# A weight load moved one step earlier in the DMA queue, and three idle products moved behind a kernel's first transposes

## The chip, the cores and the metric

The kernel runs on one core of a Trainium2 chip. A core has five engines that run their own instruction streams: TensorE (matrix products; PE, with its weight loads listed as PEld), VectorE (DVE), ScalarE (ACT), GpSimd (POOL) and SyncE (SP), which in this kernel issues all DMA transfers of the main part. The metric is the device time of one execution in microseconds (us); less is better. Times inside the program are counted from the start of the profiled span.

## The reference

The reference is a stack of two transformer layers on `x` of shape (16, 256, 256), with a condition vector per sample (16, 256) and a context (16, 256, 192). Everything is float32.

```python
# layer 0: 16 heads of width 64, rotary positions on q and k
attn_in = adaln(x, cond, ...)              # layernorm * (1 + cond@gw) + cond@bw
x = attn(attn_in, attn_in, ...) + x        # self attention
cross_in = adaln(x, cond, ...)             # the same modulation again
x = attn(cross_in, ln(context), ...) + x   # cross attention
x = gelu(adaln2(x) @ w1) @ w2 + x          # feed-forward
# layer 1: 16 heads of width 16, scale and shift from silu(cond) @ Wmod
x = x + attn(h1 @ Wqkv) @ Wos
x = x + attn(h2 @ Wq, context @ Wk, context @ Wv) @ Woc
x = x + gelu(h3 @ W1) @ W2
```

So there are six phases (layer 0: self attention, cross attention, feed-forward; layer 1: the same), each for 16 samples. A phase has its own weights.

## The kernel before, in words

**Order of work.** The 16 samples of `x` stay in SBUF for the whole run. A job is one phase of one sample: 6 x 16 = 96 jobs, phase by phase. An attention job has two steps (`s` = 0 and 1), each for half of the heads; a feed-forward job has four. One Python loop over all steps writes the instructions of every engine in the order in which they run (a manual schedule: nothing reorders them). A step holds work of several jobs at once: softmax sums and weighted sums of the current job, rotary projections of the next step, the output product of the job before, and the preparation of jobs one to three places ahead.

**One layer-0 attention step on TensorE** is, in this order: projections of keys and queries for the next step (`stage_rotary`, products recorded at L82), weighted sums of values (`layer0_sums`, L611), in step 0 the values of the next job (`layer0_values`, L82 and, for cross attention, L445 too; in step 1 the output product of the job before), and the scores of the next step (`stage_s`, L542). Behind the scores, a coming step of cross attention starts its keys (L478). DVE multiplies projections by the rotary tables (L499), POOL combines the two halves to `qk` (L507), ACT takes the exponential (L554) and copies out of PSUM (L618, L451). The helper `product` (L82) issues each product as four of 32 output rows.

**The sums of the softmax.** `sum_up` turns the row sums into reciprocals `inv` (L585), SP writes them to DRAM (`sums_seen`, L588) and reads them back spread over the partitions (`spread`, L591); POOL multiplies the raw outputs by them (L600) and forms folded sums (L709) for an output product in the manner of Strassen, whose results DVE adds to `x` (L723 to L730).

**Transfers.** All of them go through SP's one queue, strictly in program order; an instruction of SP that waits holds all behind it. A job's normalized input is transposed by DVE and turned through DRAM: `turned` (L326) out, `fetched` (L336) back; the context of cross attention goes the same way (`turned_c` L349, `fetched_c` L360), and its tile becomes `cT`.

**Weights of the next phase** come by `load_phase(p, part)`. For layer-0 attention the parts are "early" (output weights and bias), "first" and "last" (one half each of key and query weights, L228 and L229) and "values" (the value weights, two transfers of 512 KB, L236). The value weights have a single buffer (`wv`): cross attention's `wv_ca` can be written only when TensorE has read self attention's `wv_sa` for the last time. That is in `layer0_values` of the last self-attention job (b = 15), which stands in step 0 of the job before it (b = 14). The condition `leaving` holds in the two steps of the last sample of a layer-0 attention phase.

**The beginning.** `condition()` transposes the condition vectors and the table of bias rows (L154) on TensorE. Between them stand `idle_products`: products of the identity matrix (128 x 128 by 128 x 256, L136) into PSUM bank 0, whose results nobody reads. Then the first modulation (`modulation`, eight products at L175, five DVE instructions L182 to L186), four transposes of the first normalized sample (L859), and `prepare_input`, where ACT (L369) and DVE (L370) write one half each of `hT`, the input of the first projections.

Of the kernel before, what the change touches and what calls it, by code (L numbers as in the profile page):

```python
# [43 lines left out]
def fast(ctx: ExitStack, tc: tile.TileContext, a: dict, out: bass.AP, flag):  # L44
# [5 lines left out]
    NB = a["x"].shape[0]  # L50
# [13 lines left out]
    def bank(i, *inner):  # L64

        flat = banks[:, i, :]
        if len(inner) == 1:
            return flat[:, 0 : inner[0]]
        return flat[:, 0 : inner[0] * inner[1]].rearrange("p (a n) -> p a n", n=inner[1])
# [41 lines left out]
    def column(name, c):  # L111
        r, _, w = row_of[name]
        return cols[0:w, r + c : r + c + 1]
# [13 lines left out]
    def transpose_condition(s, src):  # L127
        pc = bank(5 + s, KC, NB)
        for c in range(KC):
            nc.tensor.transpose(pc[:, c, :], src[:, c * P : (c + 1) * P], ident[:NB, :NB])  # L130
        nc.vector.tensor_copy(condT[:, s], pc)

    def idle_products(n):

        for _ in range(n):
            nc.tensor.matmul(  # L136
                bank(0, 2, P), ident, ident.unsqueeze(1).to_broadcast([P, 2, P]), start=True, stop=True
            )

    def condition():  # L140

        sig = work.tile([NB, D], F32, tag="inv", name="sig")
        nc.scalar.activation(sig, cond, AF.Sigmoid)
        soon = stat.tile([NB, 1], F32, tag="ve", name="soon")
        nc.scalar.activation(soon, cond[:, 0:1], AF.Exp)
        silu = work.tile([NB, D], F32, tag="inv", name="silu")
        idle_products(1)
        transpose_condition(0, cond)
        nc.vector.tensor_mul(silu, sig, cond)
        idle_products(1)  # L150
        transpose_condition(1, silu)
        idle_products(2)
        pr = bank(4, n_rows)
        nc.tensor.transpose(pr, rows, ident[:n_rows, :n_rows])  # L154
        idle_products(1)
        return pr

    def load_modulation(shift_w, scale_w, name, between=None):
# [207 lines left out]
    def affine(pt, cw, scale, bias, tag, name, eng=nc.gpsimd):  # L366

        dst = work.tile([cw, 2, N], F32, tag=tag, name=name)
        nc.scalar.activation(dst[:, 0, :], pt[:, 0, :], AF.Identity, bias=bias(0), scale=scale(0))  # L369
        eng.tensor_scalar(dst[:, 1, :], pt[:, 1, :], scale(1), bias(1), ALU.mult, ALU.add)  # L370
        return dst
# [41 lines left out]
    def prepare_input(job):  # L413

        b, key = job["b"], job["key"]
        factor, addend = job["phase"]["mod"]
        job["hT"] = hT = affine(
            job.pop("hraw"), P,
            lambda c: factor[:, c, b : b + 1], lambda c: addend[:, c, b : b + 1], "hT", f"hT_{key}",
            nc.vector if b == 0 and job["p"] == 0 else nc.gpsimd,  # L420
        )
        if not job["cross"]:
            job["kT"] = hT
        elif job["layer"] == 0:
            job["kT"] = affine(
                job.pop("craw"), P,
                lambda c: column("L0_xcond_ca_lnc_w", c), lambda c: column("L0_xcond_ca_lnc_b", c),
                "cT", f"cT_{key}",
            )
# [368 lines left out]
    def load_phase(p, part):  # L798
        ph = phases[p]
        if part == "early" and ph["layer"] == 0 and p > 0:  # L800
            ph["make_mod"] = ph["mod_load"]() if ph["mod_load"] else lambda at: phases[p - 1]["mod"]
        ph.setdefault("w", {}).update(ph["load"](part))
# [3 lines left out]
    for p, ph in enumerate(phases):  # L806
        for b in range(NB):
            job = {"phase": ph, "p": p, "layer": ph["layer"], "kind": ph["kind"], "cross": ph["cross"], "b": b,
                   "key": f"{p}_{b}", "index": len(jobs), "qk": {}, "pr": {}, "turns": [], "raw": [], "parts": [], "halves": [],
                   "last": p == len(phases) - 1}  # L810
# [38 lines left out]


    pr = condition()
    jobs[0]["hraw"] = bank(7, KC, N)
    found = moments(xs[0], "first")
# [3 lines left out]
    for c in range(KC):  # L857
        for t in range(NT):
            nc.tensor.transpose(  # L859
                jobs[0]["hraw"][:, c, t * P : (t + 1) * P], xh[:, t, c * P : (c + 1) * P], ident  # L860
            )
    prepare_input(jobs[0])
    for e in range(2):
        for half in range(2):
# [11 lines left out]
    for i, (j, s) in enumerate(steps):  # L876
        job = jobs[j]
        ffn, layer0 = job["kind"] == "ffn", job["layer"] == 0
# [8 lines left out]
        if s == 1 and job["b"] == (3 if ffn else 1) and more:  # L887
            load_phase(job["p"] + 1, "early")
            if job["layer"] == 1:
                for part in ("first", "last"):  # L890
                    load_phase(job["p"] + 1, part)
        leaving = layer0 and not ffn and job["b"] == NB - 1
        if leaving and s == 0:
            for part in ("first", "values"):
                load_phase(job["p"] + 1, part)
        if layer0 and not ffn and s == 1 and job["b"] == 2:
            make_mod = phases[job["p"] + 1]

# [731 lines left out]
```

## Time and profile before

| what | before |
|---|---|
| device time, three runs | 2203.62, 2204.10, 2205.29 us; median 2204.1 |
| the profiled execution | 2205.85 us as timed, span 2204.0 us |
| mean granted TensorE clock in it | 0.999 of full |
| PE busy | 2186.9 us (99%) |
| DVE / POOL / ACT busy | 1663.7 (75%) / 1071.4 (49%) / 837.7 us (38%) |
| DMA | 117.69 MB, mean 53 GB/s |
| self attention of layer 0 ends, cross attention begins | near 670 to 690 us |

The profile is one execution on the chip. A row of its timeline has the start, the length, the engine, the line of the kernel, the operation with what it writes and reads (`out<-in`), shapes, and how many instructions are merged; square brackets give the engine's idle time in front and what ended it. A float32 product shows as two records, so a product by `product` (four parts) shows as eight. Rows overlap a little, since products are pipelined; the distance between starts is the safer measure. A row of a list of windows gives the length of the window, the busy time of PE, PEld, DVE, ACT and POOL in it with counts, then the granted TensorE clock, the busy share of the DMA engines and GB/s.

### The profile page before, as it was taken

What the parts mean: (1) busy time and instruction counts of PE and PEld (TensorE: products, weight loads), DVE (VectorE), ACT (ScalarE), POOL (GpSimd) and SP (SyncE); (2) the same over time, 40 slices, a digit from 0 to 9 for tenths busy, and PEclk for the clock granted to TensorE, in tenths of its full rate; (3) what the DMA queues carried; (4) which work ended last, traced back from release to release, by engine and by line L of the source; (5) the groups of instructions that cost most, each with busy time, mean ns of one, the idle gap of its engine ahead of it and who ended that gap; (6) DMA issues with size and microseconds to landing.
All of it is one profiled execution on the core that took longest, in us unless ns stands there. A gap on an engine that the chain in (4) does not pass through costs nothing.

```text
span 2204.0 us, 110738 instructions
## 1 busy us (share of the span) xinstructions
PE 2186.9 (99%) x50501; PEld 1460.3 (66%) x50501; DVE 1663.7 (75%) x3116; ACT 837.7 (38%) x1303; POOL 1071.4 (49%) x1033
## 2 busy tenths in 40 slices
PE   9999999999999999999999999999999999999998
PEld 5666666666655666666665667776656566558998
DVE  5886776776787898889899875554777777777654
ACT  3323323323323323333333332224666666663322
POOL 3766656666656867676776751221232332322220
PEclk9999999999999999999999999999999999999999
DMA  6110110111132221222212123221222232223221
GB/s 191 46 40 22 25 40 22 24 40 22 28 82 72 66 61 39 50 50 42 58 34 60 25 72 87 49 45 28 65 42 42 50 96 60 61 51 86 61 63 36
DMA packets 306248, 117.69 MB, mean 53 GB/s; under 512 B 242580, under 2 KB 289001, under 8 KB 305641
## 3 DMA queue, kind: packets, MB, share of 16 engines
q1 hardware_dynamic: 305768, 110.51, 21.0%
q8 instruction: 397, 6.50, 1.3%
q14 instruction: 83, 0.67, 0.1%
HBM read 77.14 MB, written 33.29 MB: 50 GB/s over the span
## 4 chain that ended last, share of the span: by engine, by line
PE 95%; POOL 1%; DVE 1%; DMA 1%; issue 1%; ACT 0%; SPq 0%; DVEq 0%; POOLq 0%; ACTq 0%
PE banks L82 62%; PE banks L542 16%; PE banks L611 9%; PE banks L627 5%; PE banks L478 1%; PE banks L445 1%; POOL raw L600 1%; PE banks L175 0%; DVE m L499 0%; POOL qk L507 0%; DMA sums_seen<-inv 0%; POOL folded L709 0%; ACT pr L554 0%; DMA rows<-in_rows 0%; DMA spread<-sums_seen 0%
## 5 line engine op out<-in xcount | busy, mean ns | idle before, releaser
L554 ACT ACTIVATE pr<-banks 128x1024 f32<-128x1024 f32 x576 | 487.8, 937 | 411.3 <-PE banks L542 207.9
L507 POOL TENSOR_TENSOR qk<-m,m 128x512 f32<-128x512 f32 x256 | 347.6, 1378 | 305.3 <-DVE m L499 208.1
L499 DVE TENSOR_TENSOR m<-banks,rope 128x512 f32<-128x512 f32 x512 | 324.0, 678 | 81.1 <-POOL qk L507 75.4
L563 DVE TENSOR_TENSOR both<-pr 128x512 f32<-128x512 f32 x256 | 224.6, 890 | 109.9 <-ACT pr L554 109.4
L618 ACT COPY raw<-banks 128x512 f32<-128x512 f32 x128 | 75.2, 587 | 473.4 <-PE banks L611 467.3
L542 PE MATMUL banks<-qk 32*64 32x256 f32 x8192 | 241.5, 378 | 2.3 <-DVE x L726 1.4
L611 PE MATMUL banks<-pr,v 128*32 128x256 f32 x4096 | 233.2, 379 | 0.0
L542 PEld LDWEIGHTS banks<-qk 32*64 32x64 f32 x8192 | 184.9, 131 | 63.0 <-issue 23.2
L677 ACT ACTIVATE g<-banks,cols 128x256 f32<-128x256 f32 x256 | 107.2, 471 | 294.4 <-PE banks L82 275.7
L611 PEld LDWEIGHTS banks<-pr,v 128*32 128x32 f32 x4096 | 133.1, 110 | 88.4 <-ACT pr L554 0.7
L600 POOL TENSOR_TENSOR raw<-raw,spread 128x512 f32<-128x512 f32 x128 | 164.2, 1317 | 21.1 <-DMA spread<-sums_seen 15.0
L82 PE MATMUL banks<-folded_w,folded 128*32 128x128 f32 x5856 | 173.1, 273 | 0.0
L569 DVE STREAM_TRANSPOSE squares<-both 128x1024 f32<-128x1024 f32 x128 | 159.4, 1246 | 4.4
L82 PEld LDWEIGHTS banks<-folded_w,folded 128*32 128x32 f32 x5856 | 162.5, 110 | 0.1
L576 DVE TENSOR_REDUCE rows<-squares 128x32 f32<-128x1024 f32 x128 | 155.4, 1214 | 2.2
L662 POOL TENSOR_TENSOR oT<-oT,spread 128x256 f32<-128x256 f32 x64 | 45.8, 738 | 210.7 <-DVE spread L661 210.7
L303 POOL TENSOR_TENSOR rstd<-ve,neg_half 128x2 f32<-128x2 f32 x95 | 75.3, 792 | 144.3 <-DVE ve L301 141.0
L82 PE MATMUL banks<-hT,wk_sa 128*32 128x256 f32 x2048 | 136.1, 384 | 0.9 <-ACT hT L369 0.9
L627 PE MATMUL banks<-pr,wide_v 128*32 128x256 f32 x2048 | 134.4, 379 | 1.1 <-ACT pr L554 1.1
L82 PE MATMUL banks<-hT,wq_sa 128*32 128x256 f32 x2048 | 134.8, 381 | 0.0
L82 PE MATMUL banks<-hT,wq_ca 128*32 128x256 f32 x2048 | 134.0, 379 | 0.0
L396 POOL TENSOR_TENSOR x<-x,bo_b 128x256 f32<-128x256 f32 x96 | 73.2, 782 | 124.5 <-DVE xh L311 124.5
(154 smaller groups left out, 3680.7 us busy)
## 6 DMA issues: line engine op xcount, KB each, us to landing
turned<-blocks SPq DMA_DIRECT2D x380, 64.0 KB
fetched<-turned SPq DMA_DIRECT2D x380, 64.0 KB
spread<-sums_seen SPq DMA_DIRECT2D x128, 128.0 KB
x<-in_x SPq DMA_DIRECT2D x16, 256.0 KB
fetched_c<-turned_c SPq DMA_DIRECT2D x64, 64.0 KB
cT<-in_ctx_turned SPq DMA_DIRECT2D x16, 256.0 KB
out<-x SPq DMA_DIRECT2D x16, 256.0 KB
ctx<-in_ctx SPq DMA_DIRECT2D x16, 192.0 KB
```

The lines of the kernel that those rows point to most:

```text
L82: nc.tensor.matmul(out[cut], lhsT[:, cut], rhs, start=start, stop=stop)
L499: nc.vector.tensor_tensor(m, pq, rope[:, s : s + 1, :].to_broadcast([P, 2, N]), ALU.mult)
L507: nc.gpsimd.tensor_tensor(r, x, y, (ALU.subtract, ALU.add)[out])
L542: nc.tensor.matmul(banks[64 * g : 64 * g + 64, at + h, t * N : (t + 1) * N], lhs, rhs, start=(half == 0), stop=(half == 1 or job["layer"] ...
L554: nc.scalar.activation(pr[:, one], sc[:, one], AF.Exp, scale=0.125 if job["layer"] == 0 else 0.25)
L563: nc.vector.tensor_tensor(job["both"][:, 2 * p : 2 * p + 2, :], pr[:, :, 0, :], pr[:, :, 1, :], ALU.add)
L569: nc.vector.transpose(job["squares"].rearrange("p b k -> p (b k)"), job.pop("both").rearrange("p h n -> p (h n)"))
L576: nc.vector.tensor_reduce(job["rows"][:, u, :], job.pop("squares"), AX.X, ALU.add)
L600: nc.gpsimd.tensor_tensor(part, part, spread[:, u : u + 1, :].to_broadcast([P, 2, N]), ALU.mult)
L611: nc.tensor.matmul(o[32 * h : 32 * h + 32, half, :], v[:, t, col : col + 32], prs[h // 2][:, h % 2, t, :], start=(t == 0), stop=(t == NT - 1),
L627: nc.tensor.matmul(o[32 * h : 32 * h + 32], v[:, t, 4 * c + h, 32 * e : 32 * e + 32], prs[h // 2][:, h % 2, t, :], start=(t == 0), stop=(t ...
L677: nc.scalar.activation(g[:, c, :], ph[:, c, :], AF.Gelu, bias=column(w["b1"], 2 * u + c))
```

## The change

Two things move; nothing is computed differently.

1. `load_phase(..., "values")` of the next layer-0 phase is now called in step 1 of the job b = 14. Before, it was called one step later, in step 0 of b = 15, together with "first". In SP's queue the two `wv_ca` transfers so stand directly behind `fetched_c` of cross attention's first job, and ahead of `turned` and `turned_c` of its second job (four transfers each) and of the first halves of the key and query weights (`wk_ca`, `wq_ca`), which they followed before. The same condition holds at the end of cross attention, where the next phase is the feed-forward, which has no "values" part, so nothing is issued.
2. The idle product that stood between the transpose of the bias rows and the first modulation is gone, and three stand between the four transposes of the first sample and the first projections.

The other engines' instructions and their order are the same.

```diff
@@ condition()
         idle_products(2)
         pr = bank(4, n_rows)
         nc.tensor.transpose(pr, rows, ident[:n_rows, :n_rows])
-        idle_products(1)
         return pr
@@ the beginning, behind the modulation
             nc.tensor.transpose(
                 jobs[0]["hraw"][:, c, t * P : (t + 1) * P], xh[:, t, c * P : (c + 1) * P], ident
             )
+    idle_products(3)
     prepare_input(jobs[0])
@@ the loop over steps
         leaving = layer0 and not ffn and job["b"] == NB - 1
+        if layer0 and not ffn and job["b"] == NB - 2 and s == 1:
+            load_phase(job["p"] + 1, "values")
         if leaving and s == 0:
-            for part in ("first", "values"):
-                load_phase(job["p"] + 1, part)
+            load_phase(job["p"] + 1, "first")
```

## The prediction

> **What bounds the kernel now.** I read the page's busy shares first, then who TensorE waits for, then the two stretches in which it stands.
>
> ```profile
> PE 2186.9 (99%) x50501; PEld 1460.3 (66%) x50501; DVE 1663.7 (75%) x3116; ACT 837.7 (38%) x1303; POOL 1071.4 (49%) x1033
> PE banks L82 <- DMA wv_ca<-in_ca_wkv: 2.9, 1, 2.9
> PE banks L542 <- DVE x L726: 1.4, 2, 0.8
> ```
>
> TensorE is busy 2186.9 of 2204.0 us, so only its 17 us of idle time and products that run slowly can be won. Its longest wait in the whole run (second line: who waited, for what, us, times, longest) is for `wv_ca`, cross attention's value weights. The timeline shows the place, and one stage later the same work without the wait:
>
> ```profile
> 653.48 0.98 SPq L236 DMA_DIRECT2D wv_ca<-in_ca_wkv x2
> 653.37 3.64 PE L611 MATMUL banks<-pr,v 128*32 128x256 f32 x64
> 659.92 4.97 PE L82 MATMUL banks<-wv_ca,cT 128*32 128x512 f32 x32 [2.92 <-DMA wv_ca<-in_ca_wkv]
> 666.70 3.71 PE L542 MATMUL banks<-qk 32*64 32x256 f32 x128
> 698.00 3.64 PE L611 MATMUL banks<-pr,v 128*32 128x256 f32 x64
> 706.87 3.71 PE L542 MATMUL banks<-qk 32*64 32x256 f32 x128
> ```
>
> From the weighted sums (L611) to the next scores (L542) the disturbed passage takes 666.70 - 653.37 = 13.33 us, the clean one 706.87 - 698.00 = 8.87. **4.46 us** are lost: 2.92 idle and about 1.5 because the products then ran slowly. Fine windows (last three columns: granted clock, DMA share, GB/s) show the clock:
>
> ```profile
> 659.00:659.50 0.50, 0.00 (x0) 0.00 (x0) 0.47 (x2) 0.00 (x0) 0.50 (x1) 0.74 1.05 406
> 660.00:660.50 0.50, 0.50 (x4) 0.13 (x8) 0.50 (x2) 0.00 (x0) 0.00 (x0) 0.50 1.06 370
> 662.50:663.00 0.50, 0.50 (x9) 0.19 (x5) 0.47 (x4) 0.00 (x0) 0.00 (x0) 0.85 0.00 0
> ```
>
> Means of 0.74 and 0.85 put the drop to one half at 659.24 and the return at 662.65.
>
> The start is slow too, though the clock column says 1.00 there:
>
> ```profile
> 6.85 1.16 PE L136 MATMUL banks<-ident 128*128 128x256 f32 x2
> 7.80 3.43 PE L175 MATMUL banks<-condT,mod_a 128*128 128x16 f32 x16
> 11.08 1.09 PE L859 MATMUL banks<-ident,xh_first 128*128 128x128 f32 x4
> 13.08 1.94 PE L82 MATMUL banks<-hT,wk_sa 128*32 128x256 f32 x16 [0.91 <-ACT hT L369]
> 17.88 1.04 PE L82 MATMUL banks<-hT,wq_sa 128*32 128x256 f32 x16
> 793.26 1.82 PE L175 MATMUL banks<-condT,mod_a 128*128 128x16 f32 x15
> ```
>
> A modulation takes 3.43 us here and 1.82 at 793 us; two projections take 1.71 (13.08 to 14.79, where the query group begins) and 0.86 after 17.88 (next group at 18.74). The projection begun at 17.35 takes 0.53, between the two, so full speed begins at about 17.56.
>
> [...] 659.24 to 662.65 is 3.41, and 659.24 - 17.56 = 641.68 is 188 times 3.413. [...] Here 16 KB of `sums_seen` issued at 655.67 let its reader go only at 662.16 (6.50 us in the chain), against 1.72 from issue to issue at 611.09.
>
> **Part 1, the value weights.** Two DMAs of 512 KB move ahead of ten others in SP's queue: four `turned_1`, four `turned_c_1`, `wk_ca` and `wq_ca`. Their new place is behind `fetched_c`, whose issue ends at 618.30. The load waits there for TensorE's last read of `wv_sa` in the same buffer; those products run from 615.51 until the scores at 622.49. SP's next work is `turned_1` at 645.16, so a blocked SP for 4 us holds nobody. One MB at the 300 to 400 GB/s of 657 to 661 us takes about 3 us; nothing else moves from 622.5 to 645. The data are there near 626 to 628 for a use at 656.8: 29 us to spare. The context (`cT`) is there too, its second half made at 646.39 in 0.56. The banks are free: the last evacuation of the sums ends at 657.66 (bank 5), and values take banks 6 and 7 first. Gain: **4.46**.
>
> What is late next? The stage's other long chain is also on DMA: reciprocal `inv` ready at 652.60, `sums_seen` issued at 655.67, spread from 662.22, POOL's multiply (L600) at 667.91, three foldings, `rstd`, rotary subtraction, DVE's update of x, and TensorE standing for a bank (0.60 + 0.31 us at 688.87 and 689.79, "PE banks L542 <- DVE x L726" and L730). TensorE arrives there 4.46 earlier, so the chain must move too: it costs nothing more if POOL's multiply starts by 667.91 - 4.46 - 0.91 = 662.5. It does move: the two weight issues (0.98) leave the queue, so `sums_seen` goes at about 654.6, with 1.2 MB ahead of it instead of 2.3. At the 230 to 300 GB/s seen in that stretch, from 653.5, that is 657.7 to 658.8, plus 1.0 for the small write and its signal: spread from 658.7 to 659.8. It lands 3.5 later, an estimate from 512 KB at the 225 GB/s of 614 us plus its issue. So POOL starts at 662.2 to 663.3 and the present 0.91 becomes 0 to 0.8: **gain 0.1 to 0.9; I take 0.3**. In a quiet stage POOL has 3.77 us of idle time before its next rotary work (632.34), which covers the rest of the lateness.
>
> **Part 2, the idle products.** One is taken from in front of the modulation, three are added behind the transposes. Price of one at half speed: 7.80 - 6.85 = 0.95. The modulation starts at 6.87 and not 7.80 (its weights were issued before `rows`, which is in by 6.68; that they are in too is an inference). Everything up to the transposes moves by 0.93: they end at 11.04 (11.97 before), and ACT's half of hT at 12.10 instead of 13.03. Three products last until 11.04 + 2.85 = 13.89, so the first projection comes **0.81 later** than now. Behind it stand all projections, DVE's rotary, the values; none else has a deadline there: scores at 29.16 wait for POOL's qk, done at 26.96.
>
> In return TensorE stands nowhere behind 11.04. [...] With the profiled phase [...] full speed comes at 14.15. Before: 4.48 us of half speed are 2.24 of work. After: 13.89 to 14.15 does 0.13, the other 2.11 end at 16.26. Gain 17.56 - 16.26 = 1.30. [...] mean **+0.6**. Bounds: -0.5 [...] to +1.6.
>
> **Sum.** 4.46 + 0.3 + 0.6 = 5.4 us off the profiled execution's 2204.0 span (2205.85 as timed, 1.85 around the span). The three plain runs have a median of 2204.1; I take the same amount off it: **2198.7**. Nothing else changes on DVE, ACT or POOL; with TensorE 99% busy, what it gains early stays to the end as long as its later waits hang on its own progress, as the one at 767 (0.8 + 0.3) does.
>
> **Rivals.**
> (a) The stall moves to the update of x. For it: the chain's two DMA steps are what TensorE meets next, and the present trace already shows 0.91 there. Against: two of the four 512 KB loads ahead of them leave. If POOL's multiply still started at 667.91, the stand would be 0.91 + 4.46 and only part 2 would be left: 2204.1 - 0.6 = 2203.5; at half the move, about 2201.3.
> (b) The change doesn't do what it says: the load is still issued late, or something else of that step is late (context, banks). Against: the tiles' times above. Then 2203.5.
> (c) Slower: SP, in order, blocks on the buffer's release, and `turned_1` and `sums_seen` stand behind it. From a release after about 656 (652.60 plus the 3.8 of slack) each us costs one; it must eat the 5.4 and 4.4 more, so it decides from about 666, and would give 2208.5 or more. For it: a DMA is moved in front of ten others of a strict queue. Against: the last reader in the trace ends at 622.5.
> (d) The start as in the bad phase in most runs: -0.4, so 4.46 + 0.3 - 0.4 = 4.4 and 2199.7.
>
> **Chances.** A difference of 0.2% (4.4 us) is about what a measurement can tell from none. Forecast with the good start 0.53 (2197.4 to 2199.2); (d) 0.30 (2199.0 to 2200.4); (a) 0.09; (b) 0.03; (c) 0.03; more gain than 7 us, from a chain that moves further, 0.02. Faster by over 0.2%: 0.53 + 0.02 + half of (d) and 0.03 of (a), 0.73; within: 0.24; slower: 0.03. The range that leaves out no more than 2 in 10, with the ends of the unknown costs: 2196.8 to 2201.2.
>
> **What would show it.** `wv_ca` issued near 622.5 and no wait of TensorE for it; no half clock near 659; L611 to L542 in 8.9 us. POOL's L600 of that stage some 5 us earlier, and the wait on L726 there below 0.6. First modulation product near 6.9, first projection near 13.9, full speed near 14 (or, in the bad phase, later than 16). Wrong if TensorE stands for L726 or L730 by several us, if SP holds `turned_1`, or if three idle products don't bring full speed earlier.

## The result, and the profile after

| | before | changed |
|---|---|---|
| median of 22 runs each | 2204.73 us (2201.58 to 2206.99) | 2200.59 us (2198.65 to 2203.05) |
| ratio | | 0.9981, 95% interval 0.9975 to 0.9988 |
| profiled execution, as timed / span | 2205.85 / 2204.0 us | 2200.25 / 2198.4 us |
| PE busy | 2186.9 us | 2184.9 us |

The change gains 4.1 us (2.6 to 5.5), 0.19%. The two profiled executions differ by 5.6 in their spans; how much more this is than the medians' difference, and where it lies, is told below. Between the first and the second hunk the lines of the changed kernel are lower by one (L542 became L541).

Two rows of what TensorE waits for, from the changed kernel (who, for what, us in total, times, longest):

```profile
PE banks L541 <- DVE x L725: 1.6, 2, 1.0
PE banks L541 <- DVE x L729: 0.6, 2, 0.3
```

The wait for `wv_ca` (2.9) is gone from the list. The one on DVE's update of x, 1.4 before, has become 1.6. The timeline of the changed kernel shows the load, the passage that was disturbed, and the chain behind it:

```profile
622.26 0.91 SPq L235 DMA_DIRECT2D wv_ca<-in_ca_wkv  x2
651.89 0.34 DVE L584 RECIPROCAL inv<-banks 128x32 f32<-128x32 f32 x1
653.01 3.64 PE L610 MATMUL banks<-pr,v 128*32 128x256 f32 x64
653.41 0.41 SPq L587 DMA_DIRECT2D sums_seen<-inv  x1
656.46 3.62 PE L82 MATMUL banks<-wv_ca,cT 128*32 128x512 f32 x32
658.52 2.02 SPq L590 DMA_DIRECT2D spread<-sums_seen  x4
661.89 3.71 PE L541 MATMUL banks<-qk 32*64 32x256 f32 x128
663.55 5.90 POOL L599 TENSOR_TENSOR raw<-raw,spread 128x512 f32<-128x512 f32 x4 [4.37 <-DMA spread<-sums_seen]
671.79 3.64 PE L610 MATMUL banks<-pr,v 128*32 128x256 f32 x64
681.67 1.98 PE L541 MATMUL banks<-qk 32*64 32x256 f32 x64
684.64 0.61 PE L541 MATMUL banks<-qk 32*64 32x256 f32 x2 [0.99 <-DVE x L725]
685.57 1.98 PE L541 MATMUL banks<-qk 32*64 32x256 f32 x62 [0.31 <-DVE x L729]
687.48 1.09 PE L477 MATMUL banks<-cT,wk_ca 64*64 64x256 f32 x16
```

The load is issued at 622.26, right after the last read of `wv_sa`. From the weighted sums to the next scores it is 661.89 - 653.01 = 8.88 us; it was 13.33. Two wide windows of the changed kernel (granted clock third from the end) show no slow clock any more:

```profile
655.00:660.00 5.00, 5.00 (x64) 1.77 (x56) 4.93 (x6) 1.17 (x2) 2.69 (x3) 1.00 0.52 176
660.00:665.00 5.00, 5.00 (x138) 3.25 (x142) 2.10 (x11) 3.05 (x6) 1.45 (x2) 1.00 0.81 238
```

So 4.45 us are won in this passage. Behind it more is lost than before: at the update of x TensorE stands (is held up; such a wait is called a stand below) for 0.99 + 0.31 us, where it stood for 0.60 + 0.31. The same place in the kernel before:

```profile
676.60 3.64 PE L611 MATMUL banks<-pr,v 128*32 128x256 f32 x64
686.28 1.98 PE L542 MATMUL banks<-qk 32*64 32x256 f32 x64
688.87 0.61 PE L542 MATMUL banks<-qk 32*64 32x256 f32 x2 [0.60 <-DVE x L726]
689.79 1.98 PE L542 MATMUL banks<-qk 32*64 32x256 f32 x62 [0.31 <-DVE x L730]
691.70 1.09 PE L478 MATMUL banks<-cT,wk_ca 64*64 64x256 f32 x16
```

The start, from the timeline of the changed kernel:

```profile
6.86 0.38 PE L154 MATMUL banks<-ident,rows 68*128 68x68 f32 x1 [0.50 <-DMA rows<-in_rows]
7.03 3.53 PE L174 MATMUL banks<-condT,mod_a 128*128 128x16 f32 x16
10.40 1.09 PE L858 MATMUL banks<-ident,xh_first 128*128 128x128 f32 x4
11.29 2.77 PE L136 MATMUL banks<-ident 128*128 128x256 f32 x6
13.98 1.91 PE L82 MATMUL banks<-hT,wk_sa 128*32 128x256 f32 x16
15.69 1.07 PE L82 MATMUL banks<-hT,wq_sa 128*32 128x256 f32 x16
16.59 1.04 PE L82 MATMUL banks<-hT,wk_sa 128*32 128x256 f32 x16
28.73 1.55 PE L541 MATMUL banks<-qk 32*64 32x256 f32 x48
```

The modulation follows the bias rows after 0.17 us (1.12 before). The first projection comes at 13.98, 0.90 later than before, but only the first group (15.69 - 13.98 = 1.71) is at half speed; the next takes 0.90. The first scores come at 28.73, against 29.16.

### The profile page after: what moved, and what is told of

It reads as the page before. It is cut to its first block, busy times and chain, and to the rows that moved or that the text cites. A ratio compares the mean times of both kernels' runs of the same rounds, so it can differ in the third digit from the quotient of the medians.

```text
span 2198.4 us, 110747 instructions
## 1 busy us (share of the span) xinstructions
PE 2184.9 (99%) x50505; PEld 1435.8 (65%) x50505; DVE 1662.3 (76%) x3116; ACT 836.9 (38%) x1303; POOL 1070.4 (49%) x1033
## 4 chain that ended last, share of the span: by engine, by line
PE 93%; POOL 2%; DVE 2%; DMA 1%; issue 1%; SPq 0%; ACT 0%; DVEq 0%; POOLq 0%; ACTq 0%
PE banks L82 61%; PE banks L541 15%; PE banks L610 9%; PE banks L626 5%; PE banks L477 1%; PE banks L444 1%; POOL raw L599 1%; DVE m L498 1%; POOL folded L708 1%; PE banks L174 0%; POOL qk L506 0%; DMA sums_seen<-inv 0%; DMA spread<-sums_seen 0%; ACT pr L553 0%; DMA rows<-in_rows 0%
## 5 line engine op out<-in xcount | busy, mean ns | idle before, releaser
L541 PE MATMUL banks<-qk 32*64 32x256 f32 x8192 | 240.6, 378 | 2.5 <-DVE x L725 1.6
L541 PEld LDWEIGHTS banks<-qk 32*64 32x64 f32 x8192 | 185.0, 131 | 62.2 <-issue 24.8
```

Source lines behind the costliest of these rows:

```text
L541: nc.tensor.matmul(banks[64 * g : 64 * g + 64, at + h, t * N : (t + 1) * N], lhs, rhs, start=(half == 0), stop=(half == 1 or job["layer"] ...
```

## The experiments

Two theories of the sum stood against each other at first: A, that the fetch is worth about 4 us and the idle products some tenths with a clear sign; B, that the idle products are worth nothing. Then Q, that the remaining stand at the update of x comes from the DMA queue, against P, that POOL and DVE slow each other down. All runs in one table; each ratio is to the kernel before on the same chip.

| kernel | median us (runs) | ratio | 95% interval |
|---|---|---|---|
| value weights alone | 2200.10 (14) | 0.9982 | 0.9974 to 0.9990 |
| idle products alone | 2203.16 (13) | 0.9995 | 0.9986 to 1.0003 |
| no idle products | 2199.35 (15) | 0.9978 | 0.9970 to 0.9986 |
| one idle product | 2198.65 (9) | 0.9975 | 0.9965 to 0.9985 |
| six idle products | 2200.34 (16) | 0.9981 | 0.9974 to 0.9988 |
| first halves early | 2196.79 (6) | 0.9968 | 0.9956 to 0.9980 |
| first halves early, one idle product | 2196.92 (5) | 0.9965 | 0.9951 to 0.9978 |
| first halves early, values not | 2200.18 (8) | 0.9979 | 0.9969 to 0.9990 |

### The two parts, each alone

Value weights alone: the kernel before with the last hunk of the change. Idle products alone: the changed kernel with that hunk taken back:

```diff
-        if layer0 and not ffn and job["b"] == NB - 2 and s == 1:
-            load_phase(job["p"] + 1, "values")
         if leaving and s == 0:
-            load_phase(job["p"] + 1, "first")
+            for part in ("first", "values"):
+                load_phase(job["p"] + 1, part)
```

> The kernel before with part 1 alone (the value weights' load one step earlier), the idle products as they were. Theory A (the fetch gives 4.4 us by itself and hands 0.4 back at the update of x; the idle products give about +0.6 in the mean): ratio 0.9982, 4.0 us less than before, TensorE never waits for wv_ca, clock 1.00 through 655 to 665 us, the waits on L726 and L730 at the update near 685 together 1.2 to 1.4 us. Theory B (the idle products are worth nothing or cost a little, and the fetch is the whole of the 4.1): the same or up to 0.4 us more than that. If the two parts were of one size, 2 us each, ratio 0.9991.

> The kernel before with part 2 alone (the idle products behind the modulation and transposes). Theory A: mean gain 0.6 us, ratio 0.9997 (0.9994 to 1.0000); in its trace the first projection at 13.9 to 14.0[...]; the wait of 2.9 us for wv_ca stays as it was. Theory B: ratio 1.0000 to 1.0002, since a later start takes back what earlier full speed gives.

The value weights alone gain 4.0 us (2204.56 x 0.0018; 2.2 to 5.7; the medians differ by 4.5), practically the whole change, and as theory A had it (theory B's time is so near that this run alone doesn't part the two). In that kernel's trace the passage from sums to scores takes 661.32 - 652.45 = 8.87 us, and at the update of x TensorE stands for 0.99 + 0.31 us, as expected. The idle products alone gain 1.1 (-0.7 to 3.1), an interval that holds theory A's 0.6 and theory B's 0 alike: by its time this run is inconclusive. In its trace the first projection comes at 13.25, earlier than expected, since the transpose of the bias rows comes 0.7 us earlier than in the changed kernel's (6.15 against 6.86); full speed comes at 13.53. It does show the old wait where the fetch is late again. Its timeline, and a window of it with the clock:

```profile
651.54 3.64 PE L610 MATMUL banks<-pr,v 128*32 128x256 f32 x64
658.02 1.40 PE L82 MATMUL banks<-wv_ca,cT 128*32 128x512 f32 x8 [2.85 <-DMA wv_ca<-in_ca_wkv]
665.37 3.71 PE L541 MATMUL banks<-qk 32*64 32x256 f32 x128
```

```profile
658.00:663.00 5.00, 4.80 (x32) 1.01 (x32) 2.71 (x11) 0.00 (x0) 0.00 (x0) 0.66 0.33 100
```

665.37 - 651.54 = 13.83 us, 5.0 more than the clean passage: an idle time of 2.85 and then products at a mean clock of 0.66. So the fetch's gain is two things, the wait and the slow clock that stood behind it in both traces that have the long one (13.33 and 13.83 us for the passage; the seven without any wait for `wv_ca` take 8.87 or 8.88), of which the list of waits shows only the first.

### How many idle products

Three kernels differ from the changed one only in the number behind the transposes (0, 1 or 6 and not 3):

```diff
-    idle_products(3)
+    idle_products(1)
```

> The changed kernel without the three idle products behind the transposes; the one in front of the modulation is gone as well. Theory A's own arithmetic (half the sum of the first projection's start and of the moment of full speed): first projection near 12.2[...], so 0.4 us less than the changed kernel, ratio 0.9979. Rival C [...]: up to 0.8 us more than the changed kernel, ratio 0.9985.

> The changed kernel with one idle product behind the transposes and not three. Theory A's arithmetic (time of the start = constant + half of first projection's start + half of the moment of full speed): one product ends at about 12.0, when hT is only just ready, so the first projection comes at 12.2 as without idle products, and TensorE stands nowhere, so full speed comes as early as with three: 0.6 to 0.9 us less than the changed kernel, ratio to before 0.9974 (0.9970 to 0.9979). Rival C [...]: full speed as late as without them, time as without them (0.9978) or more.

> The suspected cost doubled: the changed kernel with six idle products behind the transposes. Theory A: [...] all projections run at full speed, 1.4 us more than the changed kernel in the mean, ratio to before 0.9987. Rival: the start is covered by something else (data of the projections, DVE's rotary) and the time is within 0.4 us of the changed kernel, 0.9981.

Without any, the median is 1.2 us below the changed kernel's, with one 1.9 below; by intervals neither is clearly apart from it, and the 0.9985 and 0.9978 of rival C, for which full speed comes later with fewer than three, lie within them too. The traces say more. In each the first projection's start can be read, the moment of full speed can be worked out from the excess of the early groups over 0.86 us (a group takes 1.71 us at half speed and 0.86 at full, so half of the time spent at half speed is lost), and the first scores' start can be read:

| trace | `rows` transpose | first projection | full speed | first scores | scores - (projection + full speed)/2 |
|---|---|---|---|---|---|
| before | 6.68 | 13.08 | 17.52 | 29.16 | 13.86 |
| value weights alone | 6.15 | 12.50 | 16.24 | 28.24 | 13.87 |
| first halves early, values not | 7.33 | 13.74 | 18.46 | 29.96 | 13.86 |
| changed (three) | 6.86 | 13.98 | 15.76 | 28.73 | 13.86 |
| idle products alone (three) | 6.15 | 13.25 | 13.53 | 27.26 | 13.87 |
| first halves early (three) | 6.16 | 13.04 | at once | 26.95 | 13.9 |
| none | 6.44 | 12.00 | 16.88 | 28.30 | 13.86 |
| one | 6.17 | 11.73 | 13.55 | 26.51 | 13.87 |
| one, first halves early | 6.17 | 11.68 | 15.60 | 27.51 | 13.87 |
| six | 6.66 | 15.17 | at once | 29.08 | 13.9 |

The last column is constant to 0.05 us in ten traces. Full speed being worked out from the same groups, the column can't test the half itself; it shows that from the first projection to the first scores nothing else (data, DVE, POOL) holds TensorE up, so that the prediction's arithmetic may be used. "At once" means that full speed came while the idle products were still running: three of them took 2.51 us instead of 2.69 with the first halves early, which puts it at 12.86, and the six took 4.08 instead of 5.38, which puts it at 13.87.

These moments have a check of their own. At the end of every trace TensorE has nothing left to do (in the kernel before from 2197.3 on) and the granted clock falls to half. In the kernel with the first halves early this window holds the fall:

```profile
2193.50:2194.00 0.50, 0.00 (x0) 0.00 (x0) 0.00 (x0) 0.00 (x0) 0.00 (x0) 0.92 0.11 33
```

A mean of 0.92 puts it at 2193.92. In the kernel before, it is at 2202.06 (a mean of 0.56 from 2202.00 to 2202.50), 2184.54 us behind full speed. By the prediction's 641.68 / 188 = 3.413 that is 640 intervals, and 2184.54 / 640 = 3.4133. From full speed to the fall it is 639 of these in the changed kernel (2196.86 - 15.76 = 2181.10, with a mean of 0.93 from 2196 to 2197) and in the one with the first halves early (2193.92 - 12.86 = 2181.06), and in all ten traces a whole number to within 0.06 us. So the worked-out moments lie on one beat with the fall.

Lines from the timelines of the kernels with six products and with one show the trade:

```profile
11.09 4.15 PE L136 MATMUL banks<-ident 128*128 128x256 f32 x12
15.17 1.07 PE L82 MATMUL banks<-hT,wk_sa 128*32 128x256 f32 x16
```

```profile
10.60 1.06 PE L136 MATMUL banks<-ident 128*128 128x256 f32 x2
11.73 1.94 PE L82 MATMUL banks<-hT,wk_sa 128*32 128x256 f32 x16
13.43 1.09 PE L82 MATMUL banks<-hT,wq_sa 128*32 128x256 f32 x16
```

Six products hold the first projection up to 15.17, and all of it is then at full speed (0.89 us to the next group). One fits in the time in which `hT` is being made: the first projection comes 5.56 us behind the `rows` transpose, as without any (5.56), against 7.12 with three. In time, doubling the products was expected to cost 1.4 us more than three, and the medians differ by -0.25. The measured ratio is the rival's 0.9981; theory A's 0.9987 lies just inside the interval, so the time leans to the rival and excludes neither. The start's cost is seen in the trace; that it reaches the end in the mean over runs isn't shown.

Full speed falls differently in runs of the same form: 12.9, 13.53 and 15.76 with three products, 16.24, 17.52 and 18.46 with the old form. From the `rows` transpose to the first scores it is 22.5, 22.1 and 22.6 us in the old form, 21.9, 21.1 and 20.8 with three, 20.3 and 21.3 with one, 21.9 without, 22.4 with six. In these traces three products gain 1.1 us in the mean over the old form, and one 1.6; with two or three traces each that is an indication.

### What TensorE still stands for at the update of x

```diff
@@ loop over steps
-        if leaving and s == 0:
-            load_phase(job["p"] + 1, "first")
@@ behind the last rotary projections of a layer-0 attention step
+            if job["b"] == NB - 2 and s == 1:
+                load_phase(job["p"] + 1, "first")
```

> The changed kernel with the first halves of cross attention's key and query weights (1 MB) also loaded a step earlier, behind the last projections that read their buffers (near 633 us) and ahead of turned. Theory Q (the 1.3 us that TensorE still stands at the update of x come from sums_seen queueing behind these 1 MB): sums_seen to spread in 1.7 to 2.5 us and no more 5.1, POOL's multiply at 660 or earlier and no more 663.6, the stand on L725 and L729 of that stage 0 to 0.3 us, 1.0 to 1.3 us less than the changed kernel (ratio to before 0.9975). Rival P (POOL and DVE slow each other down there, 5.9 us for the multiply and 4.8 for three foldings against 5.0 and 3.75 in a quiet stage): the stand stays over 0.6 us and the time within 0.5 us of the changed kernel.

The kernel with the first halves early, its timeline:

```profile
650.04 0.34 DVE L584 RECIPROCAL inv<-banks 128x32 f32<-128x32 f32 x1
650.97 0.41 SPq L587 DMA_DIRECT2D sums_seen<-inv  x1
653.10 1.75 SPq L590 DMA_DIRECT2D spread<-sums_seen  x4
658.00 4.98 POOL L599 TENSOR_TENSOR raw<-raw,spread 128x512 f32<-128x512 f32 x4 [0.67 <-DMA spread<-sums_seen]
660.04 3.71 PE L541 MATMUL banks<-qk 32*64 32x256 f32 x128
669.94 3.64 PE L610 MATMUL banks<-pr,v 128*32 128x256 f32 x64
679.62 3.71 PE L541 MATMUL banks<-qk 32*64 32x256 f32 x128
683.26 1.12 PE L477 MATMUL banks<-cT,wk_ca 64*64 64x256 f32 x16
```

`sums_seen` to `spread` takes 2.13 us and no more 5.11, POOL multiplies 7.96 us after the reciprocal and no more 11.66, and the scores at 679.62 run through in one piece. Theory Q holds. P isn't what makes the difference: the three foldings are as slow here as in the changed kernel (4.65 against 4.78) and the stand is gone all the same. The multiply is quicker (4.98 against 5.90); why isn't shown, and whether POOL at its quiet pace would shorten the stand in the changed kernel wasn't tried.

By its median the gain was underrated: 1.0 to 1.3 us were expected over the changed kernel, the medians differ by 3.8. The expected ratio of 0.9975 lies within the interval, though, so the times don't settle it. The trace shows that the stand had been read too short. From the scores' start to the next keys (L477) this kernel takes 683.26 - 679.62 = 3.64 us, the changed one 687.48 - 681.67 = 5.81, and the kernel before 691.70 - 686.28 = 5.42. So behind the scores' start the stand costs 2.17 us in the changed kernel and **1.78** before, and not the 1.30 and 0.91 of the idle column. Most of the difference is that between the two idle times two records of a product count as busy for 0.61 us while all behind them waits for the second bank.

In the changed kernel some of it is paid ahead of the scores, too. From the weighted sums to the same keys it is 683.26 - 669.94 = 13.32 us here, 687.48 - 671.79 = 15.69 in the changed kernel and 691.70 - 676.60 = 15.10 before: **2.37** and 1.78 us in all. Counted so, the stand follows the start of POOL's multiply. The kernel before fixes the one constant: the stand is 10.47 us plus the multiply's start less that of the weighted sums (667.91 - 676.60 + 10.47 = 1.78), and nothing where that is negative. It gives the stand of the nine other traces, from 0 to 2.78 us, to within 0.14. So it is the late multiply, and behind it the late `spread`, that TensorE pays for.

The start is 1.8 us earlier in this kernel's trace than in the changed one's. 0.7 of it is the earlier transpose of the bias rows (6.16 against 6.86), the rest the moment of full speed; both differ between like runs, so this is luck, and how much of the medians' 3.8 it makes isn't known.

### Another order of the same loads

The kernel before, with the key and query halves moved ahead of `turned` and the value weights left where they were:

```diff
-        if leaving and s == 0:
-            for part in ("first", "values"):
-                load_phase(job["p"] + 1, part)
+        if leaving and s == 0:
+            load_phase(job["p"] + 1, "values")
...
+            if job["b"] == NB - 2 and s == 1:
+                load_phase(job["p"] + 1, "first")
```

> The kernel before, its idle products too, with the value weights at their old place in the program, and the first halves of key and query weights (1 MB) moved ahead of turned instead of them. Theory Q (what counts is how much stands ahead in the queue): wv_ca, issued at about 652, has only itself ahead, lands near 656 to 657, and TensorE waits for it 0 to 0.6 us without a half clock; sums_seen still stands behind 1 MB, so TensorE still stands about 2 us at the update of x; 3.4 to 4.4 us less than before, ratio 0.9982. Rival (the late issue itself is the cause): TensorE waits for wv_ca over 2 us, as before, ratio 0.9997 or more.

The value weights are issued at 651.88 here, only 1.6 us earlier than in the kernel before, but without 1 MB ahead of them. The timeline:

```profile
654.17 3.64 PE L611 MATMUL banks<-pr,v 128*32 128x256 f32 x64
657.72 1.07 PE L82 MATMUL banks<-wv_ca,cT 128*32 128x512 f32 x8
658.97 2.78 PE L82 MATMUL banks<-wv_ca,cT 128*32 128x512 f32 x24 [0.18 <-DMA wv_ca<-in_ca_wkv]
663.56 3.71 PE L542 MATMUL banks<-qk 32*64 32x256 f32 x128
683.16 1.98 PE L542 MATMUL banks<-qk 32*64 32x256 f32 x64
688.96 1.09 PE L478 MATMUL banks<-cT,wk_ca 64*64 64x256 f32 x16
```

The passage takes 9.39 us, 0.5 over the clean one, and from scores to keys it is 688.96 - 683.16 = 5.80, as in the changed kernel. Whichever megabyte stays there, `sums_seen` pays: it takes 4.71 us to `spread` here. The rival's forecast, a wait of over 2 us, missed. But what made `wv_ca` late this run doesn't settle: counted from the weighted sums, the issue is 2.4 us earlier than in the kernel before (651.88 - 654.17 against 653.48 - 653.37), and that alone would cut a wait of 2.92 to about 0.5. So the missing megabyte and the earlier issue, which comes with it, are not told apart.

### Both better forms together

The kernel with the first halves early, with one idle product and not three.

> The two better forms together: first halves of key and query weights early, one idle product. Theory A with Q: no stand of TensorE at the update of x near 685 us (worth 2.2 us, by the distance from the scores' start to the next keys), and 0.6 to 0.9 us of the start, so 2.8 to 3.1 us less than the changed kernel, ratio to before 0.9967 (0.9962 to 0.9972). If the two gains hid the same thing, the time would be that of the kernel with early weights alone.

Measured 0.9965 (0.9951 to 0.9978), 2196.92 us against the 0.9967 expected; the kernel with three idle products and the first halves early has 2196.79. Both beat the kernel before clearly, and their medians lie 3.7 and 3.8 us below the changed kernel's, with intervals that overlap its own a little; which of the two is better isn't settled by 5 and 6 runs. That they are so close speaks neither for nor against a gain of 0.6 to 0.9 from the single product: the moment of full speed alone moves the start by more (15.60 in the one trace, 12.86 in the other).

## Why the prediction was right or wrong

The forecast of 2198.7 us was 1.9 below the measured 2200.59; the range held it. In gain: 5.4 predicted, 4.1 (2.6 to 5.5) measured. The main mechanism was right and carries nearly all of it; the two smaller terms, taken as +0.9 together, came to about -0.2 in the traces (-0.59 and +0.43).

- **What bounds it and part 1.** 4.46 us for the passage; the two traces give 4.45. The load's issue was put at 622.5 and came at 622.26, held nobody up in SP's queue (the next issue there, `turned`, came at 644.81), and rivals (b) and (c) are out. The slow clock went with the wait (1.00 from 655 to 665 us), and came back where the wait did (0.66).
- **What is late next.** This step failed, in sign: 0.3 gained was taken, 0.59 was lost (a stand of 2.37 against 1.78 us). It had two terms. POOL's multiply was put at 662.2 to 663.3 and came at 663.55: `spread` was issued when expected (658.7 forecast, with an estimated 1.0 for the small write and its signal; 658.52 measured) but took 5.0 us to land and not 3.5, and it takes 4.9 with the first halves early as well. And the deadline of 662.5 rested on the 0.91 of the idle column; with the stand's real 1.78 it is 667.91 - 4.81 - 1.78 = 661.3 (4.81 being the scores' lead at 661.89 over 666.70, the start's gain in it). A multiply 2.2 late gives a stand of about 2.2 by this sum; 2.37 was measured. So rival (a) came true to a small part: the stand moved there, at 2.4 us and not at 5.
- **Part 2.** The prices were right: 0.95 for an idle product (1.12 to 0.17 between `rows` and modulation), 0.81 later for the first projection (0.90 in the two traces, 0.72 counted from the `rows` transpose), full speed earlier in the traces. In the profiled execution full speed came at 15.76 and not at 14.15, so 0.43 and not 1.3. The 14.15 (3.41 ahead of the 17.56 before), the mean of +0.6, the -0.4 of a bad start (half of 0.81) and their chances were the author's estimates; what brings the clock back was not shown (how busy TensorE was ahead of it stands in the last section). The mean isn't refuted (1.1, -0.7 to 3.1, alone), nor shown. What the step missed is that the number of products itself is a free choice: by the author's estimate one is better than three by 0.6 to 0.9, and none by 0.4; the times don't settle either.
- **The sum.** 4.45 - 0.59 = 3.9 agrees with the measured gain of the value weights alone (4.0, 2.2 to 5.7), and with the start's 0.43 it is 4.3 against the measured 4.1. The profiled spans differ by 5.6, and 1.1 of this is not the change's: from the scores at 941.68 to those at 1250.28 the kernel before takes 308.60 us, and all nine other traces take 0.6 to 1.2 less, though none of the experiments touches that stretch. What held that one execution up is open.
- **Chances.** 0.73 for faster by over 0.2% was more than the case bore: a gain of 0.19% lies within, and the two terms whose sign was not known were both leaned to the good side. The measured 2200.59 lies just outside the band of rival (d), between it and (a) at half the move.

## What to carry to other kernels

Price a stand by the distance between starts of the same work in a disturbed and a clean stage, not by the idle time in front of the instructions: here 0.91 shown was 1.78 paid, and 2.92 shown was 4.46, since the clock was at half from 659.24 to 662.65. Count from far enough ahead: in the changed kernel 0.20 of 2.37 us were paid in front of the scores. When a large load leaves a queue that is issued in order, look for the small transfer that stood behind it (here `sums_seen`, 6.50, 5.11 and 2.13 us to its reader) and for what large load still stands there; moving that one too was worth about half as much again in the traces (2.37 us). In the traces of this start, products whose results nobody reads were free as long as they fitted in the wait for the data, and delayed the first useful product beyond it: it came 5.56 us behind the `rows` transpose with none and with one, 7.12 with three.

## What was not expected of the hardware

- The transfer of the bias rows (34 KB) lands at different times in like runs: TensorE's transpose of them starts at 6.15 to 7.33 us. In four of the ten traces TensorE visibly waits for them (0.30 to 0.97 us), and what follows is shifted by that.
- 16 KB written to DRAM and reported back took 6.50 us behind 2.3 MB, 5.11 behind 1.2 MB and 2.13 behind 0.2 MB.
- In all ten traces the return to full speed at the start and the fall of the clock at the end are 638 to 640 times 3.4133 us apart, though the kernels do different work in between.
- How busy TensorE was in the 3.41 us ahead of a beat didn't settle in these traces whether full speed came with it. In the kernel before it was busy for 2.73 us (80%) from 659.24 to 662.65, and full speed came; for 3.10 us (91%, idle products and three small transposes of 16 and 68 columns) from 3.91 to 7.32, and the modulation behind that ran at half speed (3.43 us against 1.82). Without idle products 0.9 us of transposes and 1.5 us of projections in the 3.41 us up to 13.47 (16.88 - 3.41) didn't bring it; with the first halves early, 2.33 us of idle products and 0.89 of transposes of 128 x 128 in the 3.41 us up to 12.86 were followed by it. What makes the difference isn't shown.
